# First unit of a selective scan: its softplus sums on GpSimd and VectorE, du loaded ahead of dt, and five matmuls before the input

## The chip, the cores and the metric

The kernel runs on one core of a Trainium2 chip. The metric is device time in microseconds of one execution; for several executions the median is given. TensorE is called PE (and PEld where it loads weights), VectorE DVE, ScalarE ACT, GpSimd POOL; SP is SyncE, which here issues most DMAs. A tile is a buffer with up to 128 partitions; "128x512" is partitions by elements of a partition, all in 4-byte floats.

## The reference, cut to what matters

Two layers of a network of the MetaFormer kind act on x of shape (4, 384, 32, 32). The first is a selective scan over the image in four directions, then a mixture of experts; the second is attention, then a small feed-forward part. Only the scan is touched here:

```python
xs = _cross_scan(x)                       # x is layer-normed; 4 directions k, length L = 1024
x_dbl = einsum('bkdl,kcd->bkcl', xs, x_proj_weight)
dts, Bs, Cs = x_dbl[:, :, :12], x_dbl[:, :, 12:28], x_dbl[:, :, 28:]
dts = einsum('bkrl,kdr->bkdl', dts, dt_projs_weight)
dt = softplus(dts + dt_projs_bias)        # (4, 4, 384, 1024)
def step(h, inp):                         # over the 1024 positions
    h = h * exp(dt * A) + (dt * u) * B    # 16 states for each of 384 channels
    y = sum over the 16 states of h * C
```

So two products of the projection are needed for each channel and position: dt, which goes into the exponential, and du = dt * u, which is multiplied by B.

## The kernel before, in words

**Units and chunks.** The scan works in 32 units: 4 batches b, in each 4 directions k in the order 0, 1, 3, 2, in each two halves i of 512 positions. A unit has 3 chunks c of 128 channels. For each unit, `project` computes dt and du and writes them to a DRAM tile dd (dd[0] holds dt, dd[1] holds du), and loads the rows of B and C, broadcast to 32 partitions each, into the bcs tiles (16 DMAs, L350). `chunk` loads dt and du back in another layout: a dtr tile has, for 4 of the 16 states, 32 channels on 32 partitions each, and two such blocks of channels. A chunk has four dtr tiles of 512 KB: for q = 0 and q = 1 one of dt and one of du, each loaded by four DMAs of 128 KB (L424).

**The scan itself.** For each of 4 groups g of states and each q, POOL multiplies du by B (L440), ACT makes da = exp(dt * A) twice (L449), DVE scans twice (L454), and the product with C is done by POOL for q = 0 (L468) and by DVE for q = 1 (L461). TensorE sums the states with the matrix sel (L475). So POOL does three products of 128x1024 for each g, and the first of each needs du, while the scan needs that product and dt.

**Softplus.** `begin` (L363 to L383) makes dt before the bias in PSUM (L365). With v = dt + bias, ACT makes mag = exp(-|v|), one_e = 1 + mag, lnw = ln(one_e), the relu of v, and then 1 - one_e or one_e - 1. The sum relu + lnw + mag - (one_e - 1) is softplus with the rounding of 1 + mag repaired. It is made in one of two ways. In batch 0 (b == 0) TensorE adds four terms into the PSUM tile with identity weights (L378), four matmuls for each chunk. In later batches POOL makes two subtractions (L395, L396) and DVE an addition into PSUM (L402). Then DVE multiplies with u (L403, into the tile of one_e), ACT copies dt into the tile of mag (L404), and SP writes both to dd (L405, L406).

**Buffers.** The tiles wdt, xd, mag, one_e, lnw and relu, and the squares of a layer norm, share six buffers k2. dt's PSUM tile, the layer norm's sums and acc share two buffers "ps". There are 7 dtr buffers, 6 bx, 5 bcs, and 2 da in PSUM.

**Order of the work.** The functions are generators: the main loop (L258 to L295) advances `project` of the next unit by one step for each group of the present one. The first unit is projected ahead of the loop (L253), with nothing to overlap with but its own start: the input's first half is loaded (L222), normed (L159 to L182) and projected (L332 to L338). The order of instructions on each engine, and of DMA issues on SP, is not written by hand: the framework plans it at build time from the order of the program, priorities and simulated times (`schedule_with_timeline_sim`, L1367). Each engine then works its list in order, and an instruction that waits holds up those behind it on its engine. `place_behind` ties the POOL and DVE steps of softplus behind the last scan steps emitted before; for the first unit it is None (L251), so there they are free. `self.kept` remembers for directions 0 and 1 the DRAM tile of projected rows; the first unit puts in its first entry (L339) ahead of its softplus, the second unit its second.

**The tail.** The mixture of experts and the second layer of a batch are emitted after the scan of the next batch and fill what its scan leaves free. After the last scan only tail work is left.

Of the kernel before, what the change touches and what calls it, by code (L numbers as in the profile page):

```python
# [9 lines left out]
F32 = mybir.dt.float32  # L10
# [7 lines left out]
P = 128  # L18
# [5 lines left out]
HF = 512  # L24
# [59 lines left out]
EXACT = {"kw": 4, "k12": 2, "k4": 4, "got": 2}  # L84

FORWARD = 20000

NARROW_BANKS = {"o": 1, "p": 3}
WIDE_BANKS = {"o": 2, "p": 6}
# [22 lines left out]
def halves(i):  # L112
    return slice(i * HF, (i + 1) * HF)


class Body:
# [69 lines left out]
    def scan_layer(self, x1, between):  # L186

        nc, tc, a = self.nc, self.tc, self.a
        with ExitStack() as ctx:
# [4 lines left out]
            psum = ctx.enter_context(tc.tile_pool(name="s_ps", bufs=2, space=PSUM))  # L194
# [18 lines left out]
            def start(b):  # L213
                x = work.tile([P, DC, L], F32, tag="u", name="u")
                src = a["x"][b].rearrange("(c p) l -> p c l", p=P)
                if b > 0:
                    nc.sync.dma_start(out=x, in_=src)
                    self.layernorm(x, x, self.eps6, psum, work)
                    return x

                for i in range(NH):
                    nc.sync.dma_start(out=x[:, :, halves(i)], in_=src[:, :, halves(i)])  # L222
                self.layernorm(x, x, self.eps6, psum, work, parts=[0])
                return x

            def finish(b, y, i):
# [19 lines left out]
                for k in ORDER  # L246
                for i in (range(NH) if k < 2 else reversed(range(NH)))
            ]
            us = {0: start(0)}
            ahead = []  # L250
            self.place_behind = None  # L251
# [6 lines left out]
            for n, unit in enumerate(units):  # L258
                b, k, i = unit
                fed, ahead = ahead, []  # L260
                project = iter(())
                if n + 1 < len(units):
                    nb = units[n + 1][0]
                    if nb not in us:
                        us[nb] = start(nb)
                    project = self.project(units[n + 1], us[nb], wx, work, dram, psum, ahead)
                    next(project)
# [29 lines left out]
    def project(self, unit, u, wx, work, dram, psum, made):  # L297

        nc, a = self.nc, self.a
        b, k, i = unit
        by_cols = k % 2 == 1
        w = slice(i * (HW // NH), (i + 1) * (HW // NH))

        def rows_of(c):
            if by_cols:
                return u[:, c, :].rearrange("p (h w) -> p h w", h=HW)[:, :, w]
            return u[:, c, halves(i)]  # L310

        def to_rows(ap):
            return ap.rearrange("p (w h) -> p h w", h=HW) if by_cols else ap

        def part(c):
            if by_cols:
                return u[:, c, :].rearrange("p (h w) -> p w h", h=HW)[:, w, :]
            return u[:, c, halves(i)]

        def split(ap):  # L320
            return ap.rearrange("p (w h) -> p w h", h=HW) if by_cols else ap

        def k2(name, shape=(P, HF)):
            return work.tile([*shape], F32, tag="k2", name=name, bufs=6)

        wdt = k2("wdt", (XP, D))
        nc.sync.dma_start(out=wdt, in_=a["wdt"][k])
        xd = k2("xd", (XP, HF))
        if k < KG // 2:
            ps = psum.tile([P, HF], F32, tag="ps", name="xd_ps")  # L330
            for c in range(DC):
                nc.tensor.matmul(  # L332
                    to_rows(ps[:XP, :]), wx[:, c, k, :], rows_of(c),
                    start=(c == 0), stop=(c == DC - 1),
                )
            nc.scalar.copy(xd, ps[:XP, :])
            both = dram.tile([XP, HF], F32, tag=f"both{k}{i}", name="both")
            nc.sync.dma_start(out=both, in_=xd)  # L338
            self.kept[k, i] = both  # L339
        else:  # L340
            both = self.kept[k - KG // 2, i]
            nc.sync.dma_start(out=xd, in_=both)
        at = k // (KG // 2) * XA + R
        rows = both[at : at + 2 * NS, :]
        view = rows.rearrange("(t g n) l -> n t g l", t=2, g=NG)
        bcs = []
        for g in range(NG):
            bc = work.tile([P, 2, HF], F32, tag="bcs", name="bcs", bufs=5)
            for n in range(NJ):
                nc.sync.dma_start(  # L350
                    out=bc[n * DB : (n + 1) * DB], in_=view[n, :, g].partition_broadcast(DB)
                )
            bcs.append(bc)

        dd = dram.tile([2, D, HF], F32, tag="dd", name="dd")
        made += [bcs, dd]  # L360
        yield

        def begin(c):  # L363
            ps = psum.tile([P, HF], F32, tag="ps", name="dt_ps")
            nc.tensor.matmul(ps, wdt[:, c * P : (c + 1) * P], xd, start=True, stop=True)  # L365
            bias = self.col("dtb", k * DC + c)
            mag, one_e, lnw = k2("mag"), k2("one_e"), k2("lnw")
            relu = k2("relu") if b == 0 else ps
            nc.scalar.activation(mag, ps, AF.Abs, bias=bias)
            nc.scalar.activation(relu, ps, AF.Relu, bias=bias)  # L370
            nc.scalar.activation(mag, mag, AF.Exp, scale=-1.0)
            nc.scalar.activation(one_e, mag, AF.Identity, bias=1.0)
            nc.scalar.activation(lnw, one_e, AF.Ln)
            if b == 0:
                nc.scalar.activation(one_e, one_e, AF.Identity, bias=1.0, scale=-1.0)
                terms = [lnw, one_e, mag, relu]
                for t in terms:
                    nc.tensor.matmul(  # L378
                        ps, self.ident, t, start=(t is terms[0]), stop=(t is terms[-1])
                    )  # L380
            else:
                nc.scalar.activation(one_e, one_e, AF.Identity, bias=self.minus1)
            return ps, mag, one_e, lnw  # L383

        def behind(engine):
            if self.place_behind is None:
                return nullcontext()
            return self.tc.issue_after(self.place_behind[engine])

        for c in range(DC):  # L390
            ps, mag, one_e, lnw = begin(c)
            yield
            if b > 0:
                with behind("pool"):
                    nc.gpsimd.tensor_sub(mag, one_e, mag)  # L395
                    nc.gpsimd.tensor_sub(lnw, lnw, mag)  # L396
            yield
            d, du = mag, one_e
            rows = slice(c * P, (c + 1) * P)
            with behind("dve"):  # L400
                if b > 0:
                    nc.vector.tensor_add(ps, ps, lnw)  # L402
                nc.vector.tensor_mul(split(du), split(ps), part(c))  # L403
            nc.scalar.copy(d, ps)  # L404
            nc.sync.dma_start(out=dd[0, rows, :], in_=d)  # L405
            ins = nc.sync.dma_start(out=dd[1, rows, :], in_=du).ins  # L406
        made.append(ins)

    def chunk(self, unit, first, c, fed, carry, nega, sel, acc, work, dap):
# [3 lines left out]
        nc = self.nc  # L413
        b, k, i = unit
        bcs, dd, _ = fed
        dtr = []
        for q in range(NJ // 2):

            pair = []
            at = c * P + q * 2 * DB  # L420
            for s in range(2):
                t = work.tile([P, 2, HF], F32, tag="dtr", name="dtr", bufs=7)
                for n in range(NJ):
                    nc.sync.dma_start(  # L424
                        out=t[n * DB : (n + 1) * DB],
                        in_=dd[s, at : at + 2 * DB, :].rearrange("(j d) l -> d j l", d=DB),
                    )
                pair.append(t)
            dtr.append(pair)

        def run(ap):
# [3 lines left out]
        for g in range(NG):  # L435
# [36 lines left out]
            for q in range(NJ // 2):  # L472
                for j in range(2):
# [3 lines left out]
                        start=(g == 0), stop=(g == NG - 1),  # L477
# [28 lines left out]
    def first_layer(self, b, room):  # L506

        self.experts(b, self.slots, room)
        with self.tc.high_priority(offset=FORWARD):
            xt, xn = self.combine(b, *self.place, room)  # L510
            return self.prologue(xt, xn, room)

    def second_layer(self, b, xc, room, between):
        att = self.attention(xc, self.sums[:, b], room)
        with self.tc.high_priority(offset=FORWARD):
            self.last_layers(b, att, room, between if b < 2 else ())
# [107 lines left out]
    def route(self, b, x1, room):  # L624

        def forward():
            return nullcontext() if 0 < b < B - 1 else self.tc.high_priority(offset=FORWARD)

# [395 lines left out]
    def attention(self, xc, sums, room):  # L1024
# [68 lines left out]

        steps = [(t, i, j) for t in range(HEADS // 2) for i in range(NH) for j in range(MB)]
        made = [project(0)]
        ahead = scores(0, made[0][0], 0, 0, None)
        atts = []
# [377 lines left out]
```

## Time and profile before

| what | value |
|---|---|
| median of 3 runs | 4278.92 us (4278.86 to 4291.83) |
| profiled execution, its own time | 4300.74 us |
| its span, first to last instruction | 4299.0 us |
| mean granted TensorE clock | 0.865 |
| POOL products L440 / L468 | 768 x 2358 ns / 384 x 2357 ns |
| ACT exponentials L449 | 1536 x 690 ns |
| identity matmuls L378 | 4 for each of the 24 chunks of batch 0 |
| HBM traffic | 161 GB/s over the span |

The profile is of one execution. A row of the timeline gives start and length in us, engine, line, operation, the tile written and those read, and how often; in brackets stands how long the engine was idle before it and what ended that. TensorE's records are halves: an fp32 matmul of 128x512 shows as two. In a row of 40 slices each digit is the busy share of one fortieth of the span in tenths; PEclk is the clock that TensorE was granted. A row of waits gives the engine and line that waited, for what, the sum in us, how often, and the longest.

### The profile page before, as it was taken

The numbers are of one execution on the slowest core, as the hardware profiler recorded it, in microseconds if no ns is written. First come the engines' busy times: TensorE is split into PE (matmuls) and PEld (weight loads), VectorE is DVE, ScalarE is ACT, GpSimd is POOL, SyncE is SP. The second block draws the span as 40 slices with busy tenths as digits, with TensorE's granted clock in tenths as the row PEclk, the third lists the DMA queues.
The fourth block names the chain that finished last, engine by engine and source line by source line (L and its number), as shares of the span: only waits on it lengthen the run. The fifth ranks groups of instructions, "written<-read, shape, count | busy, mean of one in ns | idle before, by whom it ended". The sixth has DMA issues, their size and how long they took to land. (4 is left out here: it accounts for less than half of the span.)

```text
span 4299.0 us, 45575 instructions
## 1 busy us (share of the span) xinstructions
PE 3329.5 (77%) x13244; PEld 1560.8 (36%) x13244; DVE 2852.0 (66%) x4200; ACT 2516.4 (59%) x4486; POOL 3020.0 (70%) x1471
## 2 busy tenths in 40 slices
PE   6445444389897888589985889579896889998896
PEld 2111111155553223145652223135553225566322
DVE  5998997878786867788786878878887820010101
ACT  5555545556665775666664777666665654343354
POOL 5999997898898968789898978888989810000100
PEclk8666666689998999589997999679998999999997
DMA  5454563577795535578886434558789243345100
GB/s 140 128 124 122 135 170 107 168 220 224 229 276 158 137 113 142 169 207 236 239 257 191 114 101 140 158 173 237 234 236 272 77 158 100 121 143 202 50 26 19
DMA packets 410322, 693.69 MB, mean 161 GB/s; under 512 B 51024, under 2 KB 209616, under 8 KB 410064
## 3 DMA queue, kind: packets, MB, share of 16 engines
q1 hardware_dynamic: 400752, 664.29, 53.4%
q0 software_dynamic: 8192, 25.17, 1.8%
q8 instruction: 106, 1.74, 0.2%
q14 instruction: 152, 1.25, 0.1%
q10 hardware_dynamic: 1120, 1.25, 0.1%
HBM read 569.00 MB, written 121.50 MB: 161 GB/s over the span
## 5 line engine op out<-in xcount | busy, mean ns | idle before, releaser
L440 POOL TENSOR_TENSOR bx<-dtr,bcs 128x1024 f32<-128x1024 f32 x768 | 1791.8, 2358 | 181.1 <-PE acc L475 93.6
L449 ACT ACTIVATE da<-dtr,nega 128x512 f32<-128x512 f32 x1536 | 1045.5, 690 | 928.7 <-DVE bx L461 580.8
L468 POOL TENSOR_TENSOR bx<-bx,bcs 128x1024 f32<-128x1024 f32 x384 | 903.7, 2357 | 154.6 <-DVE carry L465 67.3
L475 PE MATMUL acc<-bx,sel 128*32 128x512 f32 x3072 | 493.5, 701 | 306.4 <-POOL bx L468 261.0
L941 PE MATMUL h_ps<-xc,w 128*128 128x256 f32 (+1 forms) x3168 | 663.5, 365 | 47.7 <-DVE xc L928 17.4
L956 PE MATMUL y_ps<-w,hs 128*128 128x384 f32 x1824 | 644.6, 507 | 52.5 <-ACT hs L949 52.5
L941 PEld LDWEIGHTS h_ps<-xc,w 128*128 128x128 f32 x3168 | 551.2, 198 | 218.9 <-issue 93.7
L454 DVE TENSOR_TENSOR_SCAN bx<-da,carry,bx 128x512 f32<-128x512 f32 x384 | 473.8, 1270 | 114.7 <-ACT da L449 64.4
L454 DVE TENSOR_TENSOR_SCAN da<-da,carry,bx 128x512 f32<-128x512 f32 x384 | 476.1, 1273 | 77.5 <-ACT da L449 62.1
L454 DVE TENSOR_TENSOR_SCAN bx<-da,bx 128x512 f32<-128x512 f32 x384 | 453.7, 1211 | 90.9 <-ACT da L449 54.3
L461 DVE TENSOR_TENSOR bx<-da,bcs 128x512 f32<-128x512 f32 x768 | 509.8, 679 | 3.0
L454 DVE TENSOR_TENSOR_SCAN da<-da,bx 128x512 f32<-128x512 f32 x384 | 455.5, 1219 | 76.5 <-ACT da L449 53.0
L956 PEld LDWEIGHTS y_ps<-w,hs 128*128 128x128 f32 x1824 | 353.0, 197 | 337.4 <-issue 71.7
L1071 ACT ACTIVATE ex<-s_ps 128x512 f32<-128x512 f32 x512 | 300.3, 591 | 164.2 <-PE s_ps L1065 148.4
L1065 PE MATMUL s_ps<-w 64*128 64x512 f32 x1024 | 305.1, 659 | 68.5 <-ACT ex L1071 64.4
L977 POOL TENSOR_TENSOR diag<-ident,g_weight 128x1024 f32<-128x1024 f32 x8 | 15.1, 1903 | 443.1 <-PE xc_ps L924 430.0
L1111 PE MATMUL o_acc<-ex,vt 128*64 128x512 f32 x1024 | 286.1, 638 | 24.6 <-ACT ex L1071 18.5
L946 ACT ACTIVATE hs<-h_ps,bb 128x256 f32<-128x256 f32 (+1 forms) x528 | 199.9, 440 | 174.9 <-PE h_ps L941 170.9
L475 PEld LDWEIGHTS acc<-bx,sel 128*32 128x32 f32 x3072 | 76.2, 116 | 603.9 <-POOL bx L468 373.3
L960 DVE TENSOR_TENSOR y<-y_ps,bb 128x384 f32<-128x384 f32 x76 | 41.6, 548 | 250.6 <-PE y_ps L956 250.6
L365 PE MATMUL dt_ps<-xd,wdt 108*128 108x512 f32 x192 | 123.6, 731 | 73.0 <-ACT mag L404 48.3
L1065 PEld LDWEIGHTS s_ps<-w 64*128 64x128 f32 x1024 | 81.8, 189 | 269.1 <-ACT ex L1071 222.6
(218 smaller groups left out, 3593.3 us busy)
## 6 DMA issues: line engine op xcount, KB each, us to landing
w<-in_w SPq DMA_DIRECT2D x352, 576.0 KB
dtr<-dd SPq DMA_DIRECT2D x1536, 128.0 KB
bcs<-both SPq DMA_DIRECT2D x512, 128.0 KB
dd<-one_e SPq DMA_DIRECT2D x96, 256.0 KB
dd<-mag SPq DMA_DIRECT2D x96, 256.0 KB
rows<-zero SPq DMA_DIRECT2D x76, 192.0 KB
xt<-x SPq DMA_DIRECT2D x32, 384.0 KB
xs<-rows SPq DMA_DIRECT2D x32, 384.0 KB
```

What stands on the lines that cost most here:

```text
L440: pool = nc.gpsimd.tensor_mul(bx, dtr[q][1], bc[:, 0].unsqueeze(1).to_broadcast([P, 2, HF])).ins
L449: nc.scalar.activation(da, dtr[q][0][:, j, :], AF.Exp, scale=nega[:, col : col + 1])
L454: nc.vector.tensor_tensor_scan(run(h), run(da), run(bx[:, j, :]), 0.0 if first else hold, ALU.mult, ALU.add,)
L461: dve = nc.vector.tensor_mul(bx[:, j, :], h, cg).ins
L468: pool = nc.gpsimd.tensor_mul(bx, bx, cg.unsqueeze(1).to_broadcast([P, 2, HF])).ins
L475: nc.tensor.matmul(acc[lo : lo + DB, :], sel, out[q][:, j, :], start=(g == 0), stop=(g == NG - 1),)
L941: nc.tensor.matmul(ps[:, r, :], w1[(f + r) // wf][:, c, (f + r) % wf * P : ((f + r) % wf + 1) * P], xc[:, c, :], start=(c == 0), stop=(c = ...
L946: nc.scalar.activation(hs[:, f + r, :], ps[:, r, :], AF.Identity, bias=bb[:, f + r : f + r + 1])
L956: nc.tensor.matmul(out[:, :D], hs[:, f, t * P : (t + 1) * P], w2[f // wf][:, f % wf, :], start=(f == 0), stop=(f == FC - 1),)
L1065: ins = nc.tensor.matmul(ps, w[rows, j * P : (j + 1) * P], w[rows, halves(i)], start=True, stop=True).ins
L1071: done.append(nc.scalar.activation(ex[:, o, :], ps, AF.Exp, scale=HD**-0.5, accum_out=sums[:, t, 2 * j + o, i : i + 1],).ins)
L1111: ins = nc.tensor.matmul(out[cols, :], made[t][1][:, j, cols], ex[:, o, :], start=(j == 0), stop=(j == MB - 1),).ins
```

## The change

A constant WARM = 5 is new. Ahead of the first load of x in program order, five matmuls of the ones matrix with itself (repeated to 512 columns) go into a "ps" tile that nothing reads.

The choice between the two ways of softplus no longer asks whether b is 0, but whether b is 0 and `self.kept` has more than one entry. At the first unit it has one, at every later unit two or more. So the first unit alone changes over, to POOL and DVE; it then needs no relu tile, since relu stays in PSUM.

In `chunk`, of each pair of dtr tiles the one of du (s = 1) is allocated and loaded before the one of dt (s = 0), for all 96 chunks. The pair is indexed as before.

```diff
+WARM = 5
...
+            warm = psum.tile([P, HF], F32, tag="ps", name="warm")
+            for _ in range(WARM):
+                nc.tensor.matmul(
+                    warm, self.ones, self.ones.unsqueeze(1).to_broadcast([P, HF // P, P]),
+                    start=True, stop=True,
+                )
             us = {0: start(0)}
...
+        by_products = b == 0 and len(self.kept) > 1
+
         def begin(c):
...
-            relu = k2("relu") if b == 0 else ps
+            relu = k2("relu") if by_products else ps
...
-            if b == 0:
+            if by_products:
                 nc.scalar.activation(one_e, one_e, AF.Identity, bias=1.0, scale=-1.0)
...
-            if b > 0:
+            if not by_products:
                 with behind("pool"):
                     nc.gpsimd.tensor_sub(mag, one_e, mag)
                     nc.gpsimd.tensor_sub(lnw, lnw, mag)
...
-                if b > 0:
+                if not by_products:
                     nc.vector.tensor_add(ps, ps, lnw)
...
-            pair = []
+            pair = [None, None]
             at = c * P + q * 2 * DB
-            for s in range(2):
+            for s in (1, 0):
                 t = work.tile([P, 2, HF], F32, tag="dtr", name="dtr", bufs=7)
...
-                pair.append(t)
+                pair[s] = t
```

## The prediction

> **What bounds the kernel now.** I read the page's summary and its 40 slices first, then tables of busy time by stretch, then the timeline of the first 62 us, and last the lists of waits.
>
> ```profile
> PE 3329.5 (77%) x13244; PEld 1560.8 (36%) x13244; DVE 2852.0 (66%) x4200; ACT 2516.4 (59%) x4486; POOL 3020.0 (70%) x1471
> POOL 5999997898898968789898978888989810000100
> PEclk8666666689998999589997999679998999999997
> ```
>
> Four stages are seen here: a start, a first batch in which POOL has nines, a long middle in which scan and tail overlap, and from slice 32 an end (some 890 us) in which POOL and VectorE are nearly idle. The table by stretches gives the limits:
>
> ```profile
> 150.00:200.00 50.00, 27.70 (x86) 7.53 (x84) 46.71 (x49) 31.41 (x51) 50.00 (x22) 0.77 0.43 119
> 300.00:350.00 50.00, 25.16 (x78) 6.09 (x70) 45.07 (x49) 28.09 (x46) 50.00 (x22) 0.67 0.51 128
> 900.00:1300.00 400.00, 363.80 (x1605) 228.72 (x1598) 326.81 (x445) 267.12 (x423) 355.61 (x165) 0.95 0.82 239
> ```
>
> The columns are busy us of PE, PEld, DVE, ACT and POOL, then clock, DMA share and GB/s. From about 120 to 650 us POOL is busy without a gap, so whatever brings its first products forward moves that whole stage. From 900 us POOL (89%) and PE (91%) share the limit, and nothing there passes one to one into the end. The start is in the timeline:
>
> ```profile
> 5.90 5.24 PE L166 MATMUL ln_mean<-u,ones 128*128 128x512 f32 x6 [5.90 <-DMA u<-in_x]
> 12.59 2.84 PE L179 MATMUL ln_var<-ln_sq,ones 128*128 128x512 f32 x6 [0.88 <-ACT ln_sq L175]
> 27.07 0.63 ACT L375 ACTIVATE one_e<-one_e 128x512 f32<-128x512 f32 x1
> 32.65 0.69 DVE L403 TENSOR_TENSOR one_e<-dt_ps,u 128x512 f32<-128x512 f32 x1 [13.93 <-issue]
> 33.37 0.35 SPq L406 DMA_DIRECT2D dd<-one_e  x1
> 33.98 0.34 SPq L405 DMA_DIRECT2D dd<-mag  x1
> 37.67 5.49 SPq L424 DMA_DIRECT2D dtr<-dd  x12
> 44.34 2.36 POOL L440 TENSOR_TENSOR bx<-dtr,bcs 128x1024 f32<-128x1024 f32 x1 [42.15 <-DMA dtr<-dd]
> 45.24 0.34 SPq L406 DMA_DIRECT2D dd<-one_e  x1
> 49.40 2.35 POOL L468 TENSOR_TENSOR bx<-bx,bcs 128x1024 f32<-128x1024 f32 x1 [2.71 <-DVE carry L465]
> ```
>
> POOL waits 42.15 us for its first operand, then 2.71 us more. Only this stretch, and what the load order does later, can move the time.
>
> **The change part by part.** *Warm-up matmuls.* Before, a TensorE record of 128x512 takes 5.24/6 = 0.87 us in the first mean and 2.84/6 = 0.47 us in the variance. Five matmuls are ten records. They can start once ones is set (about 1.2 us), and x is there at 5.9. All at 0.87 they last 8.7 us, to 9.9, and the mean behind them at 0.44 ends at 12.5 against 11.14 now: a loss of 1.4. The rule that bears on it is in the Trainium skill, "TensorE: Matmul & The Clock Gate", Part 1: about 3.4 us of sustained work, seen in a free-running window, lift the clock. By it the fast state comes between 4.6 and 8.0 us, the ten records end between 7.2 and 9.0, and the mean ends between 9.8 and 11.6: a gain of 1.3 to a loss of 0.4. The rows agree with a ramp (the granted clock is 0.50 at 18 to 20 us, after a pause of 2.15 us, and 1.00 at 22 to 24), but none shows ramp time from a cold start at 1.2. I take a gain of 0.3, the middle, with ends -1.4 and +1.3. What hides the warm-up is the wait for x; where it lasts past 5.9, x waits for it.
>
> *Softplus of the first unit.* For each of 3 chunks it removes 4 identity matmuls (eight records) and adds two POOL subtractions and one VectorE addition. For chunk 0, ScalarE ends at 27.70 (27.07 + 0.63) and the sums end at 32.55 (31.53 + 1.02): 4.85 us. The near row for the new steps is that of later batches:
>
> ```profile
> L395 POOL TENSOR_TENSOR mag<-one_e,mag x72: 1253/1272/1382, 698.9 to 3305.5; 128x512 f32<-128x512 f32 x72
> L402 DVE TENSOR_TENSOR dt_ps<-dt_ps,lnw x72: 670/689/700, 708.2 to 3340.1; 128x512 f32<-128x512 f32 x72
> ```
>
> 2 x 1.27 + 0.69 is 3.23, with hand-overs 3.35: the product du comes 1.5 us earlier. A rule speaks against POOL: "GPSIMD Engine Reference", Engine selection, puts elementwise work with two inputs on VectorE, about twice as fast. The rows agree (1.27 against 0.69); by it both subtractions on VectorE would save another 1.2 us, if this step set the pace. It doesn't, by what follows: the 16 broadcast loads of bcs are issued from 25.22 to 32.59, and the DMA share is 0.98 from 26 to 36 us and 0.47 from 36 to 38. The two dd writes, of 33.37 and 33.98, move in its last part and land by 37.6. Issued 1.5 us earlier they still stand behind those loads. So I put the gain of this step at the path at 0 (ends 0 and 1.5): its cover is the bcs traffic. Without that cover it would be worth 1.5.
>
> Chunks 1 and 2: six subtractions are 7.6 us of POOL work in all. Following the k2 buffers (six; wdt and xd hold two until the third dt matmul), I get the subtractions of chunk 1 at 34.9 to 37.4 and of chunk 2 at 39.5 to 42.1. POOL is idle until its first product, so only the last touch the path: 0.2 us, ends 0 and 2.5. What queues behind them on POOL is that product; VectorE's additions wait for them, with nothing else to do before 44. The 24 removed records give TensorE time that it doesn't need.
>
> *Load order.* It reverses pairs in all 96 chunks; the DMAs stay the same in number and size. In the first chunk du's four loads, at 5.49/12 = 0.46 us each, no longer stand behind dt's four (1.84 us), and du's write was issued 0.6 us ahead of dt's. POOL's first product comes 2.4 us earlier, at 41.9. dt now lands about when du did (44.0); with 0.69 of exponential the first scan starts near 44.8 instead of 46.73. The du tile of the second pair was fourth and stood behind the write of 45.24; as third it is issued in the first run, so POOL's second product can fill the idle 2.71 us. I take 1.6 of it (ends 0 and 2.7), because VectorE is dense from 54 us on and POOL waits for it there 4.8 us more.
>
> Sum at the start: 0.3 + 0 - 0.2 + 2.4 + 1.6 = 4.1 us earlier; with all ends at their worst (and 1.8 for the order, see the rivals) a loss of 2, at their best a gain of 8. In batch 0 behind it POOL waits for no load, so the order gives nothing there. Later:
>
> ```profile
> POOL bx L440 <- DMA dtr<-dd: 26.7, 10, 7.3
> ACT da L449 <- DMA dtr<-dd: 12.3, 8, 2.7
> SPq L424 <- ACT da L449: 208.4, 56, 21.0
> ```
>
> These are the waits of 900 to 3100 us. With seven dtr buffers and four tiles a chunk, the fourth tile waits for the previous chunk: now du for ScalarE's last use of a dt, then dt for POOL's last use of a du, which is earlier. Where loads come just in time, the scan's start was du's second place plus 2.36 and becomes dt's second place plus 0.69, up to 1.7 us better. Cutting each POOL wait in the timeline up to 3400 us by at most 2.3 us (four loads of 128 KB at 226 GB/s, the rate of 26 to 36 us) gives 17 us at most. Because PE shares the limit, and after such waits POOL makes up to seven products in a row (it catches up), I take a third, 5 us.
>
> In all 9 us of the profiled execution's 4300.7 (span 4299.0 and 1.7 around it), to 4291.7 or 0.21% less. It was 0.5% above the median of the runs, 4278.9; the same share of that gives 4270.
>
> **The rivals.** *The order pays in full*: 4 at the start and all 17 later, 4258. For it: du is what POOL waits for. Against: PE is at 91%. *Nothing comes through*: VectorE, at 98% from 60 to 70 us, has the same scans to do and eats the advance, or warm-up and cold clock cost what the rest gains: 4279. For it: POOL's waits for carry up to 120 us; against: the scan itself starts earlier. A variant is that du's loads wait for both halves of dd, so that the order wins 1.8 instead of 2.4.
>
> *Slower*: dt becomes last, and SP's in-order queue makes it late. Each dt tile is issued 4 x 0.425 = 1.7 us later. Where du was already in time, that delays ScalarE's da, then the scan, then POOL's second product. The price is 1.7 us for each of the 72 chunks of batches 1 to 3 where it bites; it decides from 13 chunks on (22 us, the 9 gained and 13 over the line). In 15 chunks it is 25 us, 4279 - 4 + 25 = 4300. It speaks for it that ScalarE already waits for dtr 8 times; against, that its waits are short and three of four tiles are loaded a chunk ahead. The planner, which lays out each engine's order from simulated times, may also deal later work anew; I have no row for it, and it widens the range only.
>
> **How the numbers follow.** A measurement of this kernel can tell about 0.3% (12.8 us) from no change: below 4266.1 is faster, above 4291.8 slower. The likeliest case, 4270 (4264 to 4276), has 0.45; order in full, 4258 (4250 to 4264), 0.27; nothing through, 4279 (4276 to 4283), 0.16; slower, 4300 (4286 to 4315), 0.12. Faster gets the full case and a fifth of the likeliest, 0.36; slower nearly all of the last, 0.11; within 0.3% the rest, 0.53. The range 4252 to 4288 leaves out most of the slower case and the low end of the full one, under 0.2.
>
> **What would show it.** In the new profile: the first POOL product near 42 us; the two dd writes of chunk 0 landing at 37 as before, though issued near 32; ln_mean's records near 0.44 us; L395 75 times; POOL without a gap from about 117 us; POOL's waits for dtr after 900 us below 26.7 us, and ScalarE's not above 30. I am wrong if the first product comes at 44 or later, if the end of batch 0 has not moved by 2 to 6 us, or if waits for dt in ScalarE have grown by over 20 us.

## The result, and the profile after

| what | before | after |
|---|---|---|
| median of 6 runs, taken together | 4288.3 us (4278.86 to 4292.33) | 4319.43 us (4313.63 to 4330.31) |
| ratio to before, 95% interval | | 1.0079 [1.0061, 1.0097] |
| profiled execution, its own time | 4300.74 us | 4313.63 us |

The change makes the kernel 31 us slower; 4270 was forecast, with 4288 as the upper end. The two profiled executions lie only 12.9 us apart: before's lies 12 us above its median, after's is the lowest of its six. So the pair of traces shows where time goes, and sizes are taken from medians.

Of the page after, the summary and POOL's row of the 40 slices:

```profile
PE 3305.3 (77%) x13230; PEld 1561.3 (36%) x13230; DVE 2848.1 (66%) x4203; ACT 2517.2 (58%) x4486; POOL 3027.3 (70%) x1477
POOL 5999998889888978889899788889888810000100
```

POOL has six instructions more, as the edit says. Its row reads 99999 in slices 2 to 6 as before; since a 9 is anything from 90% up, a loss of a few per cent in the first batch can hide there. The table by stretches, its columns as before, shows it:

```profile
150.00:200.00 50.00, 28.72 (x78) 9.16 (x78) 42.63 (x44) 27.88 (x47) 44.57 (x21) 0.73 0.32 95
900.00:1300.00 400.00, 366.63 (x1585) 230.60 (x1586) 327.22 (x441) 257.81 (x410) 355.85 (x165) 0.94 0.79 225
```

From 150 to 200 us POOL was busy for all 50 us and is now busy for 44.57; the shared stretch from 900 us is as it was. From 150 to 640 us POOL's busy time falls from 486.14 to 462.06 us. The start, meanwhile, went well. Its timeline after (start, length, engine, line, operation):

```profile
17.45 2.83 PE L339 MATMUL xd_ps<-u,wx 128*108 128x512 f32 x6 [2.15 <-DVE u L183]
30.54 0.69 DVE L412 TENSOR_TENSOR one_e<-dt_ps,u 128x512 f32<-128x512 f32 x1
31.26 0.35 SPq L415 DMA_DIRECT2D dd<-one_e  x1
34.95 5.49 SPq L433 DMA_DIRECT2D dtr<-dd  x12
39.28 2.34 POOL L449 TENSOR_TENSOR bx<-dtr,bcs 128x1024 f32<-128x1024 f32 x1 [0.20 <-DMA dtr<-dd]
```

The first product comes at 39.28 us instead of 44.34. But counted by products, that lead is soon gone. POOL does 1152 products of the scan, 36 a unit: the 36th ends 3.5 us later than before, the 252nd (seven units) 27.6 us later, at 666.1 instead of 638.5. Below, "lag" is this difference at the 252nd product. One thing must be kept in mind with it: it is counted from a single execution of before, 12 us above the median, with a slow start. e6, e11 and e12 below, which leave start, batch 0 and POOL's order there as in before, stand at -3.8 to -4.8. So of a lag of -7, some 3 us belong to an edit, not 7.

The cause is in the order of POOL's list. These are rows of its timeline in batch 0, first of before, then of after:

```profile
331.73 6.98 POOL L440 TENSOR_TENSOR bx<-dtr,bcs 128x1024 f32<-128x1024 f32 x3
338.68 2.33 POOL L468 TENSOR_TENSOR bx<-bx,bcs 128x1024 f32<-128x1024 f32 x1
340.98 4.67 POOL L440 TENSOR_TENSOR bx<-dtr,bcs 128x1024 f32<-128x1024 f32 x2
```

```profile
337.26 13.92 POOL L449 TENSOR_TENSOR bx<-dtr,bcs 128x1024 f32<-128x1024 f32 x6
351.14 4.66 POOL L477 TENSOR_TENSOR bx<-bx,bcs 128x1024 f32<-128x1024 f32 x2
356.63 2.35 POOL L477 TENSOR_TENSOR bx<-bx,bcs 128x1024 f32<-128x1024 f32 x1 [0.83 <-DVE bx L463]
363.48 13.91 POOL L449 TENSOR_TENSOR bx<-dtr,bcs 128x1024 f32<-128x1024 f32 x6 [4.50 <-PE acc L484]
```

Before, a product with C follows after one to three with B; after, the planner has put six with B and then three with C, in all units from the second to the seventh of batch 0. I call these the mixed order and bursts. The change does not write this order; it came out of the new planning. The waits from 150 to 640 us (engine, line, for what: sum in us, how often, longest), POOL and VectorE after, then VectorE before:

```profile
POOL bx L449 <- PE acc L484: 21.1, 6, 4.5
DVE bx L463 <- POOL bx L449: 27.6, 18, 2.3
```

```profile
DVE bx L454 <- POOL bx L440: 1.1, 3, 0.6
```

The prediction's view was that POOL is never held up here. Now it waits 21.1 us for a bx buffer in six places, one a unit, and VectorE 27.6 us, in 18 places, for products of a burst.

### The profile page after: what moved, and what is told of

Same layout as the page of the kernel before. It is cut to its first block, busy times and chain, and to the rows that moved or that the text cites. A ratio compares the mean times of both kernels' runs of the same rounds, so it can differ in the third digit from the quotient of the medians.

```text
span 4311.9 us, 45654 instructions
## 1 busy us (share of the span) xinstructions
PE 3305.3 (77%) x13230; PEld 1561.3 (36%) x13230; DVE 2848.1 (66%) x4203; ACT 2517.2 (58%) x4486; POOL 3027.3 (70%) x1477
```

## The experiments

Seventeen kernels were run. All times are medians; ratios are to before, measured beside it on the same chip, with 95% intervals; after and the groups e1 to e4, e5 to e8, e9 to e12, e13 to e16 and e17 were measured apart. "Anew" means that the planner laid out the order afresh. "Held" means that the program is written down twice, and in the second the engines' instructions of a part of the run are chained, in their issue order alone, into the order that the first was planned in; no wait is added.

| run | edits | batch 0 on POOL | later order | ratio | lag, us |
|---|---|---|---|---|---|
| after | all | bursts | anew | 1.0079 [1.0061, 1.0097] | +27.6 |
| e1 | softplus, warm-up | mixed | anew | 0.9998 [0.9990, 1.0007] | -7.5 |
| e2 | du first | mixed | anew | 1.0060 [1.0041, 1.0080] | -9.5 |
| e3 | all | forced mixed | anew | 1.0007 [0.9997, 1.0017] | -7.1 |
| e4 | none | forced bursts | anew | 1.0014 [1.0003, 1.0025] | +25.9 |
| e5 | all, du first in batch 0 alone | bursts | anew | 1.0049 [1.0032, 1.0067] | +28.2 |
| e6 | du first in batches 1 to 3 | mixed | anew | 1.0043 [1.0027, 1.0060] | -3.8 |
| e7 | as e5 | forced mixed | anew | 1.0013 [1.0002, 1.0024] | -7.8 |
| e8 | warm-up | mixed | anew | 1.0027 [1.0015, 1.0039] | -6.0 |
| e9 | as e5 | bursts | held to before's | 1.0057 [1.0038, 1.0077] | +27.5 |
| e10 | as e5 | forced mixed | held to before's | 0.9996 [0.9986, 1.0006] | -7.9 |
| e11 | as e6 | mixed | held to before's | 0.9993 [0.9982, 1.0004] | -4.6 |
| e12 | as e6 | mixed | held to after's | 1.0017 [1.0007, 1.0027] | -4.8 |
| e13 | as e5 | bursts of 4 and 2 | held to before's | 1.0103 [1.0085, 1.0122] | +31.9 |
| e14 | all | forced mixed | held to before's | 0.9978 [0.9969, 0.9986] | -8.7 |
| e15 | all | forced mixed, all batches | anew | 0.9941 [0.9919, 0.9963] | -6.9 |
| e16 | none | forced mixed, all batches | anew | 0.9983 [0.9973, 0.9992] | -4.7 |
| e17 | as e9 | bursts, acc ahead on TensorE | held to before's | 1.0029 [1.0017, 1.0040] | +17.3 |

**Which edit: e1, e2.** e1 is after with the loads in the old order, e2 is before with only the pairs reversed.

```diff
-            for s in (1, 0):
+            for s in (0, 1):
```

> The changed kernel with dt loaded ahead of du again, so only the first unit's softplus and the warm-up remain. Three theories. BURSTS: the slowdown comes from POOL's planned order in batch 0, which in the changed kernel is six products with B and then three with C, and it cost 27.6 us up to the 252nd scan product of POOL (638.5 us before, 666.1 after). LATE DT: dt behind du arrives late, ScalarE and then the scan wait. RE-DEALT TAIL: the tail work of batches 1 to 3 is planned anew and this alone makes the time. Without du first the planned order of POOL is mixed again. BURSTS expects the 252nd product at 634 to 638 us and a ratio to the kernel before of 0.995 to 1.001. LATE DT expects the same here. RE-DEALT TAIL expects the ratio to be anything, unrelated to the 252nd product.

> The kernel before with du loaded ahead of dt and nothing else. The planned order of POOL in batch 0 is mixed (two products with B, one with C), not in bursts. BURSTS expects the 252nd scan product of POOL by 638 us, POOL without gaps from 150 to 650 us, and a ratio of 0.995 to 1.002. LATE DT expects the loss to come with this edit alone: ScalarE's waits for dtr over 20 us more than before and a ratio of 1.005 to 1.010.

Both keep a mixed order, with lags of -7.5 and -9.5 us, some 3 and 5 below those of e6, e11 and e12. So bursts need the load order together with at least one of the other two edits; which one was not run. Yet e2 ends 0.6% slower, with batch 0 ahead: something else costs time later.

**The order alone: e3, e4.** e3 is after with the mixed order forced in batch 0: each product with B for q = 0 is issued behind the last product with C but one.

```diff
+                if b == 0 and q == 0 and len(self.pool_c) > 1:
+                    hold_back = self.tc.issue_after(self.pool_c[-2])
+                else:
+                    hold_back = nullcontext()
+                with hold_back:
                     pool = nc.gpsimd.tensor_mul(
...
+                    self.pool_c.append(pool)
```

e4 is before with bursts forced from the second unit of batch 0 on, with edges of issue order (order_only) that put every first of six behind the last product with C, and three of these behind the sixth.

```diff
+                turn = len(self.pool_c) % 3
+                burst = b == 0 and unit != (0, 0, 0)
+                if burst and q == 0 and turn == 0 and self.pool_c:
+                    hold_back = self.tc.issue_after(self.pool_c[-1])
...
+                if burst and q == 1 and turn == 0:
+                    for c_ins in self.pool_c[-3:]:
+                        self.tc.add_manual_dep(c_ins, pool.name, order_only)
```

> The changed kernel with all its edits, and in batch 0 each group's first product with B placed behind the product with C of two groups earlier in POOL's order, so that the order is two and one. Nothing else is touched. BURSTS expects the 252nd scan product at 633 to 638 us instead of 666.1, POOL's waits for acc from 150 to 650 us near 0 instead of 21, and a ratio to the kernel before of 0.996 to 1.002 (it gives back about 30 us of the 31). LATE DT expects 666 us and a ratio of 1.006 or more, as loads are as in the changed kernel. RE-DEALT TAIL expects batch 0 to gain and the ratio to stay above 1.004.

> The kernel before, its loads, softplus and start untouched, with POOL's order in batch 0 from the second unit on set to six products with B and then three with C. BURSTS expects the 252nd scan product at 658 to 668 us instead of 638.5, with VectorE waiting for POOL's first product of each burst (some 1.8 us, four times a unit), and a ratio of 1.004 to 1.009. LATE DT expects 638 us and a ratio within 0.2% of 1.

In batch 0 the order alone moves the lag from +27.6 to -7.1, and without any of the edits the bursts put it at +25.9. POOL's timeline in e3 has the form of before's again:

```profile
317.13 4.72 POOL L455 TENSOR_TENSOR bx<-dtr,bcs 128x1024 f32<-128x1024 f32 x2
321.76 2.40 POOL L483 TENSOR_TENSOR bx<-bx,bcs 128x1024 f32<-128x1024 f32 x1
```

But e4 as a whole is only 0.14% slower: forcing one part makes the planner lay out the rest anew, and there some 20 of the 26 us came back. The whole time of an edit then mixes its price with that of a new order.

**Where the load order is reversed: e5, e6, e7, e8.** e5 is after and e7 is e3 with du first in batch 0 alone; e6 is before with du first in batches 1 to 3; e8 is before with only the five matmuls.

```diff
-            for s in (1, 0):
+            for s in ((1, 0) if b == 0 else (0, 1)):
```

> The changed kernel, but du is loaded ahead of dt only in batch 0; in batches 1 to 3 dt is first again. POOL's planned order in batch 0 is in bursts as in the changed kernel. Two causes are now weighed for the 0.79%: BURSTS (the 27 us lost in batch 0 reach the end) and DU LATER (the load order in batches 1 to 3 costs it, since with du first the kernels gave 1.0079, 1.006 and, with the order of batch 0 mended, 1.0007, and with dt first 0.9998 and 1.0014). BURSTS expects the 252nd scan product near 666 us and a ratio of 1.006 to 1.009. DU LATER expects 666 us too, but a ratio of 1.000 to 1.003. LOTTERY (the planner deals the work of batches 1 to 3 anew at each edit, whatever it is) expects any ratio from 0.999 to 1.008.

> The kernel before with du loaded ahead of dt in batches 1 to 3 only; start and batch 0 are untouched, also in their planned order. BURSTS expects the 252nd product at 638 us and a ratio of 0.997 to 1.002. DU LATER expects 638 us, ScalarE's waits for dtr from 900 to 3400 us at 30 to 40 us against 14.5, and a ratio of 1.004 to 1.008. LOTTERY expects any.

> All edits, with POOL's order in batch 0 held at two and one, and du first in batch 0 only. BURSTS expects the 252nd product at 631 us and a ratio of 0.998 to 1.001. DU LATER expects the same product and a ratio of 0.996 to 1.000, at or below the run with du first everywhere and the order mended (1.0007). LOTTERY expects any.

> The kernel before with the five warm-up matmuls and nothing else. In the changed kernel the first mean ended 0.1 us earlier and the first projection, then at full clock, 1.8 us earlier, so the real gain at the start is 0 to 2 us, with the 252nd product at 634 to 638 us. BURSTS and DU LATER expect a ratio of 0.999 to 1.000. LOTTERY expects a ratio off by up to 0.5% either way, though no instruction of batches 1 to 3 is other than before except in its place.

With bursts the later load order adds 0.3% (e5 to after), with the mixed order it adds nothing (e7 to e3). And e8, whose only added work is over at 7.59 us and which is not behind in batch 0 (-6.0), is 0.27% slower. Such sizes can't be told from the price of a new order, so the order was held from here on.

**Order held: e9 to e12.** In e9 and e10 all edits act in batch 0, and every engine's order from batch 1 on is that of before (but for a few neighbours). e9 keeps the bursts, e10 has the mixed order of e3. e11 has du first in batches 1 to 3 in before's order, e12 the same in after's later order. In the diff, plan lists the positions in the program in the planned order of the first trace, and order_only is an edge of issue order.

```diff
+    for at in plan:
+        ins = traced[at + more]
+        before = last.get(str(ins.engine))
+        if before is not None:
+            tc.add_manual_dep(ins, before.name, order_only)
+        last[str(ins.engine)] = ins
```

> All three edits in batch 0, with POOL in bursts as in the changed kernel, while from batch 1 on each engine's order is held to the one planned for the kernel before (issue order only, no new waits; dt first there). The warm-up alone gave 1.0027, so a new deal of the later order alone moves the time by about 0.3%, and holding it takes this out. BURSTS expects the 252nd product near 666 us (28 us late), the lag to stay to the end, and a ratio of 1.004 to 1.007. LOTTERY alone as the cause expects a ratio of 0.999 to 1.002, the lag being absorbed where PE sets the pace.

> As the run before it, with POOL's order in batch 0 held at two products with B and one with C. This is the change as the prediction took it, with the rest of the order unchanged. BURSTS expects the 252nd product at 631 us (7 us early) and a ratio of 0.998 to 0.9995. LOTTERY as the cause of all expects the same, 0.998 to 1.000; the difference to the run before it is the pure price of the bursts.

> The kernel before with du ahead of dt in batches 1 to 3, in the places in SP's order that dt and du loads had, and with every engine's later order held. DU LATER (dt behind du is late and costs time by itself) expects ScalarE's waits for dtr at 30 to 40 us and a ratio of 1.003 to 1.006. LOTTERY (the 1.0043 of du first in later batches came from the new deal) expects 0.998 to 1.001, and POOL's waits for dtr below the 30.4 us of before.

> The reverse: start and batch 0 of the kernel before, and from batch 1 on each engine's order held to the one planned for the changed kernel, with du first there. The 252nd product is at 638 us. LOTTERY and DU LATER expect a ratio of 1.002 to 1.005, which with the batch 0 part adds up to the 1.0079. BURSTS alone expects 0.999 to 1.001.

e9 against e10 is the price of the bursts alone: 1.0057 - 0.9996 = 0.61%, 26 us. The two traces say the same: e9's products come 35.5 us behind e10's at the 252nd and 27 to 29 us behind from the 9th unit to the last, so most of it is never made up. e11 refutes the slower rival of the prediction and, with it, the theory that dt's late loads cost time: reversed loads in a held order cost nothing that shows (0.9993), where the same edit with the order made anew (e6) had 1.0043. e12 gives after's later order 0.17%. Together 0.57% + 0.17% = 0.74%, of after's 0.79% [0.61, 0.97]; the sum takes it that the two parts add.

**What a burst costs: e13, e17.** e13 has the rule of e4 with GROUPS = 2, which makes bursts of four and two and leaves two of the six bx buffers free; e17 is e9 with each engine's list as it was, but in six places of batch 0 four acc matmuls of TensorE stand ahead of the four identity matmuls of softplus.

```diff
-                turn = len(self.pool_c) % 3
+                turn = len(self.pool_c) % GROUPS
```

```diff
+        if what == "dt" and then == "acc" and rank[dve] < rank[du] and seen > 400:
+            runs[n], runs[n + 1] = runs[n + 1], runs[n]
```

> As the run with all edits in batch 0 and the rest held (1.0057), but POOL's order in batch 0 from the second unit on is four products with B and then two with C, so that two of six bx buffers stay free. If full bx buffers make the price, POOL's waits for acc from 150 to 640 us fall from 21 to near 0, the 252nd product is at 635 us or earlier and the ratio 0.998 to 1.001. If VectorE runs dry behind the products with C, VectorE still waits for the first product of a burst and the 252nd product is at 645 to 660 us, the ratio 1.001 to 1.005.

> This is e9 (all three edits in batch 0, bursts on GpSimd, later order held) with every engine's list as in e9, except that on TensorE, in six places of batch 0, four acc matmuls (the last group of a chunk) stand ahead of the four identity matmuls of softplus instead of behind them. In e9 GpSimd waits at just these six places, 21.2 us in all from 150 to 640 us, for a bx buffer that such an acc matmul still holds. BURSTS HELD BEHIND SOFTPLUS: the price of the bursts is TensorE's in-order list; GpSimd's waits for acc fall under 6 us, the 252nd scan product comes 8 to 14 us later than before instead of 27.5, and the ratio is 1.002 (1.000 to 1.004) against e9's 1.0057. ALTERNATION: the bursts cost by letting GpSimd and VectorE run out of input in turn, whatever TensorE does; when these waits go, others take their place as in e13: the lag stays above 22 us and the ratio above 1.0045.

In e13 POOL's waits for a buffer are gone, and the kernel is slower still: POOL waits for VectorE, VectorE for POOL (20.2 us), and VectorE for TensorE's finished acc sums (25.4 us at one line, 7.7 in e9). Its list of waits from 150 to 640 us has, for POOL's products with C:

```profile
POOL bx L501 <- DVE carry L498: 17.6, 12, 5.4
POOL bx L501 <- DVE bx L487: 13.2, 10, 4.8
```

e17 looks at the six buffer waits. In after, TensorE's timeline ahead of POOL's wait of 4.50 us reads:

```profile
355.66 2.08 PE L387 MATMUL dt_ps<-lnw,ident 128*128 128x512 f32 x2 [5.97 <-ACT lnw L382]
...
362.26 1.07 PE L484 MATMUL acc<-bx,sel 128*32 128x512 f32 x8
```

The acc matmuls that free the buffer stand in TensorE's list behind softplus's, which wait 5.97 us for ScalarE. In e17 they run first, at the same place:

```profile
352.22 1.94 PE L503 MATMUL acc<-bx,sel 128*32 128x512 f32 x8 [4.09 <-POOL bx L495]
354.11 2.08 PE L399 MATMUL dt_ps<-lnw,ident 128*128 128x512 f32 x2
```

```profile
357.38 4.67 POOL L467 TENSOR_TENSOR bx<-dtr,bcs 128x1024 f32<-128x1024 f32 x2
362.33 9.28 POOL L467 TENSOR_TENSOR bx<-dtr,bcs 128x1024 f32<-128x1024 f32 x4 [0.28 <-PE acc L503]
```

The second fence is POOL's timeline: its next burst starts at 357.38 without a wait, and 0.28 us is left of the 4.50. Its waits for acc fall from 21.2 (e9) to 2.8 us, its waits for scans rise from 6.8 to 12.4, VectorE's waits for POOL fall from 27.6 to 15.0. The lag falls by 10.2 us, the ratio by 0.28%. Neither theory's numbers held: the lag of 17.3 lies above the 8 to 14 of the one and below the 22 of the other. So TensorE's in-order list is a part of the price: 10 us by the lags, 8 of the 28 us by which e9 trails e10 to the end, and 12 of the 26 by the medians (the intervals of e9 and e17 just overlap). What makes the rest is not shown. In e13, where POOL finds free buffers, the price is no lower, but VectorE's waits for acc leave TensorE in play there too. More bx buffers were not tried.

**What the edits are worth: e14, e15, e16.** e14 has all three edits, the mixed order in batch 0, and before's later order held. e15 is after with the rule of e3 in all batches, e16 is before with that rule.

```diff
-                if b == 0 and q == 0 and len(self.pool_c) > 1:
+                if True and q == 0 and len(self.pool_c) > 1:
```

> All three edits, du first in all batches, POOL's order in batch 0 held at two and one, the later order held to that of the kernel before. Its parts gave 0.9996 (batch 0) and 0.9993 (du first later). If they add, 0.998 to 0.9995; if the late stage absorbs any gain, 0.9995 to 1.001.

> The changed kernel with each group's first product with B behind the product with C of two groups earlier in all batches, the later order dealt anew. BURSTS expects no loss in batch 0 and perhaps a gain where bursts in later batches (runs of three on the mean, up to six) starve VectorE: 0.995 to 1.001. LOTTERY expects 0.998 to 1.004.

> The kernel before with that same rule for POOL in all batches, later order dealt anew. If shorter runs help in the later batches, 0.995 to 0.999; LOTTERY expects 0.998 to 1.004.

With the order held, the three edits gain 0.22% [0.14, 0.31]; their two parts, e10 and e11, add up to 0.11%. e15, at 4263.80 us, beats both kernels: 0.59% [0.37, 0.81] below before, where the rule alone (e16) gives 0.17%. The difference between e15 and e14, which have the same edits, is again one of planned order, whose inner causes I didn't separate.

## Why the prediction was wrong

**The failed step** is "In batch 0 behind it POOL waits for no load, so the order gives nothing there." That POOL waits for no load is still true; that the order of loads changes nothing there is not. Together with the other edits it changed the planned order of POOL, and e9 against e10 prices that at 26 us. The prediction had named the way: "The planner, which lays out each engine's order from simulated times, may also deal later work anew; I have no row for it, and it widens the range only." It thought of later work, not of batch 0, gave it no size and no case of its own. Why the planner chose bursts stays open; e4 shows that they are slow without any edit of the change.

**The rest of the sum.** The forecast was 0.21% less; e14, where the order is held, gives 0.22%. That the two agree so well is in part luck: e10, with the start alone, gave 0.04% where 4.1 us are 0.10%, e11 with the later loads 0.07% where 5 us are 0.12%. The single terms of the start, from the traces:

| term | predicted, us | measured |
|---|---|---|
| warm-up, at ln_mean's end | 0.3 gain | 0.1 in after (11.02 for 11.14); 0.2 by the means, 10.61 in 12 traces with it, 10.82 in seven without |
| warm-up, at the projection | none | 1.7 against before (2.83 for 4.52), none against e11 (2.83) |
| softplus, chunk 0, at the du product | 1.5 | 0.3: 10.26 behind the projection's end (e1), 10.56 (e8) |
| softplus, chunk 0, at the first product | 0 | 0: 41.68 (e1) against 41.52 (e8) |
| du ahead of dt, at the first product | 2.4 | 3.0: 18.8 to 19.2 behind the projection's end in 11 traces, 21.8 to 22.3 in the eight without |
| second product, behind the first | 1.6 | 0.5: 4.5 for 5.0, by the means of the same traces |
| first product of POOL | at 41.9 | at 39.28 |
| first scan | at 44.8 | at 42.33 |

In after the clock stepped up at 6.69 us, inside the 4.6 to 8.0 us that the prediction drew from the Trainium skill, "TensorE: Matmul & The Clock Gate", Part 1 (in the twelve traces with the warm-up, 4.81 to 7.03). The prediction missed the projection behind the next pause, which is slow in before, but not for want of a warm-up: e11, e12 and e16 have none, take 2.83 us there, and make their first product at 41.87 to 41.96. So of the 5.1 us by which after's first product is early, 3.2 come behind the projection, from the load order, and 1.8 from before's slow execution; the last section shows why that one was slow.

The softplus term was sized wrongly, though it cost nothing. The sums take 3.33 us (27.07 to 30.40), close to the 3.35 said, but they start later: in e1 ScalarE works on chunk 1 before chunk 0's last step, so POOL starts at 26.20 where TensorE starts at 24.51 in e8. And 4.85 us for the old way was its time at a lowered clock: in e11, at a clock of 1.00 throughout, the du product comes 8.85 us behind the projection's end, earlier than in any trace with the edit. The cover holds: in every trace SP issues the last load of bcs, ahead of the du write, 10.1 us behind the projection's end, and e11's early du product gains nothing at the first product (22.07, against 22.10 in e8). So the advice of the Trainium skill, "GPSIMD Engine Reference", Engine selection, to give such sums to VectorE would by this have brought nothing at the first product, though the rows keep its ratio (1.26 against 0.70 us); no run tried it. The last subtraction of chunk 2 ran at 55.16, behind five products, and not ahead of the first.

The lead at the first product did not last. At the 36th product, one unit on, the kernels with all edits and the mixed order (e3, e7, e10, e14, e15) are 2.8 to 4.5 us ahead of before, e8 and e1, without du first, 5.3 and 4.7.

**Later loads.** The term of 5 us from POOL's later waits rests on the list of 900 to 3100 us. POOL's 26.7 us are gone from the list after, as predicted. ScalarE's, 12.3 in before and not above 30 by the prediction, are at the line in after and well over it in the fastest kernel, yet only 12.6 in e3, which has all edits too; the rows are of after, e11 and e15:

```profile
ACT da L458 <- DMA dtr<-dd: 29.6, 13, 6.1
```

```profile
ACT da L472 <- DMA dtr<-dd: 26.6, 7, 13.3
```

```profile
ACT da L464 <- DMA dtr<-dd: 40.8, 15, 11.6
```

These waits change hands rather than end, how many there are goes with the planned order, and no cost of them shows: e15 has the most and is the fastest. e11 against 1 gives this term a gain of 0.07% [-0.04, 0.18], 3 us for the 5 predicted, and it can't be told from none.

**The rivals.** The slower one had the right sign by the wrong mechanism: it priced dt's lateness, which e11 refutes. "Nothing comes through" fits e1, e3 and e10, whose lags of -7 to -8 us don't show in the median. In e10 most of that is before's own slow trace: counted from e11, whose batch 0 is before's, it leads by 3.4 us at the 252nd product, and its median is 0.04% [-0.06, 0.14] lower, up to 6 us. In e14 a gain did come through.

**The tests.** Two of the signs that the prediction set itself spoke: batch 0's end moved by 27.6 us the wrong way, not 2 to 6 earlier, and POOL had gaps from 150 us on. The first product, at or past 44 in the failing case, did not speak, nor did ScalarE's waits, which grew by 17.3 us in after where 20 was the sign.

## What to carry to other kernels

Where a planner lays out each engine's order, an edit has two prices: its own, and that of the order which the planner makes of it. Compare the order of the busiest engine in both traces first, by the runs of equal rows in its timeline; then hold the order to price the edit. Here the mixed order, with the later order held, turned 0.79% slower into 0.22% faster. A rule that alternates the two kinds of product on the busiest engine gave 0.17% alone and 0.59% with the change. And a lag counted from one trace carries that trace's own luck: compare with several traces that leave the stretch as it was.

## What I had not expected of the hardware

The projection L332 (L339 after), behind a pause of 2.15 us of TensorE, takes either 2.83 us or 4.4 to 4.5 us for the same six records. It is fast in all twelve traces with the warm-up; without it, slow in before, e4 and e6 and fast in e2, e11, e12 and e16. The granted clock (third number from the end) goes with it; the stretch from 18 to 20 us of before, then of after:

```profile
18.00:20.00 2.00, 2.00 (x3) 0.61 (x3) 0.72 (x2) 0.00 (x0) 0.00 (x0) 0.50 0.00 0
18.00:20.00 2.00, 2.00 (x6) 0.69 (x4) 0.59 (x1) 0.00 (x0) 0.00 (x0) 1.00 0.00 0
```

The trace's clock has two values, 1.00 and 0.50, and in before it changes only at multiples of 3.41 us behind its first step (but for one piece). Cut into stretches of that length, the whole trace of before gives a plain picture: behind a stretch with over 1.96 us of idle TensorE the clock was never kept at 1.00, and behind one with over 0.61 us it never rose. (Ends of matmuls are modelled, so these sizes are rough.) In before, e4 and e6 the stretch that ends about when the projection starts, at 17.6, 18.5 and 17.1 us, holds 2.06 to 2.15 us of idle time, nearly the whole pause, and the clock falls to 0.50 for 3.41 us. In the other sixteen traces the stretches from the first step up to there hold at most 1.92 us. So what counts is how the pause lies to the stretches. With the warm-up that step came at 4.81 to 7.03 us, and the fall never came at the projection; whether it can is not shown. In the warm-up itself the records start 0.85 us apart before the step and 0.43 behind it.

The place of a few matmuls in TensorE's in-order list was worth some 8 to 12 us (e9 to e17), on an engine that was busy for less than half of that stage (222.93 of 490 us in e9).
